# Linear attention emitted with neighbouring chunks turn by turn, constant rows filled by transfers, experts at an even rate

## The chip, the cores and the metric

The kernel runs on one core of one Trainium2 chip. The metric is the device time of one execution in microseconds (us). A core has a matmul engine (PE, its weight loads are shown as PEld), a vector engine (DVE), an activation engine (ACT), a general engine (POOL) and a queue from which this kernel starts all its transfers (SP). Each of them works through its own instructions in a fixed order and waits for the others by semaphores.

## The reference

x has the shape (4, 1024, 128): 4 sequences of T = 1024 tokens with 128 channels. Four layers follow one another; each reads a layer norm of x, and its output is added to x after a layer norm:

```python
x = x + _layernorm(_L0_attn_ref(_layernorm(x), ...))   # "A": time mixing by a scan, channel mixing
x = x + _layernorm(_L0_ffn_ref(_layernorm(x), ...))    # "B": 16 small experts, 4 per token, and a shared one
x = x + _layernorm(_L1_attn_ref(_layernorm(x), ...))   # "C": linear attention with decaying states
x = x + _layernorm(_L1_ffn_ref(_layernorm(x), ...))    # "D": softmax attention and 8 experts, 2 per token
```

Layer C is what the change is about. Per head (16 heads of 8 channels) and per time step it keeps two states M with decays b:

```python
M = M * b_t[:, :, None, None] + (k_t[:, :, None] * v_t[:, None, :])[:, None]
Z = Z * b_t[:, :, None] + k_t[:, None, :]
num = einsum('bd,bcde->be', q_t, M);  den = einsum('bd,bcd->b', q_t, Z) + EPS
y_t = num / den
```

## The kernel before

Channels lie on the 128 partitions, tokens along the free axis. The work of each layer is cut into chunks of 512 tokens, two per sequence, eight in all.

**Order of the work.** Stage A comes first, then stage B (the experts of the first feed-forward layer) beside stage C for sequences 0 and 1, then stage D, which is written out by hand and in which stage C of sequences 2 and 3 runs in between. The text is written as Python generators: each `yield` ends one step, and a driver takes steps from several generators in turn. Outside the hand-written last part the framework orders the instructions of each engine itself: the order of the text is a priority, and an instruction whose inputs and buffers are ready by the framework's own estimate may be put ahead of earlier text. Inside the last part the text order is the engine's order.

**Stage B.** `experts_b` gives 20 steps per sequence, ten per chunk; nine of the ten begin one expert: gate projection (`g_ps`, PE), clamp (L471, DVE), three activations (L473 to L475), two multiplications on POOL (L480 with the fetched routing weight, L481), the second projection (`u_ps`) with a product on DVE (L491), the third projection (`y_ps`, L464). Routing weights are fetched by one transfer per expert into three buffers (`gate`, L479). `STEPS_B = 10` of the 80 steps are written during stage A; the others are written by `with_experts` beside C and the heads of D: each "scans" step adds 0.28 to a count and each other step 0.1, and whenever the count passes 1 one expert step is written.

**Stage C**, `stage_c(b, pp, banks)`, per chunk:
- the front: the layer norm into `n2` (L573; one buffer), the projection v, written to memory as `v_rows` (L581), q and k with a rotation (`u` L588, `w` L591, sum on POOL L598, then `phi` L609) and the two decays `beta` (L596 to L610). The rotation table `turn` has a buffer of its own, fetched in one transfer of 512 KB (L569);
- the scans: for e in 8, 0, ..., 7 a product `kv` on POOL (L622, from a fetched row group `vrep`, three buffers, L618), two scans on DVE (L628), the sum of the two states on POOL (L638), a product with q on DVE (L642), and sums over partitions on PE (`den_ps` L668, `num_ps` L679);
- the tail: output projection (`o_ps` L690), `hh` (L693, in the buffer of `u`), two layer norms (L698, `ho` L704 in the buffer of `w`, L709), the sum into x (L712).

In this part of the kernel `beta` and `q` lie in three PSUM banks of their own; the other projections of C and of the heads share two PSUM banks (`room_c`).

**Ahead of D.** `keys_r` and `queries_r` (two tiles each) have constant rows 64 to 127, filled by POOL (L823, L824). `heads(b, h)` makes q, k and v of stage D, `spread(b, h)` moves them into place with 18 transfers.

The order written is: C of sequence 0 with experts (L795), the constants, heads and spread of sequence 0 for both chunks (L1237, L1238), C of sequence 1 with experts (L1239), what is left of the experts, stage D.

Of the kernel before, what the change touches and what calls it, by code (L numbers as in the profile page):

```python
# [11 lines left out]
FP = mybir.dt.float32  # L12
# [27 lines left out]
def sandwich(ctx: ExitStack, tc: tile.TileContext, x, vecs, cmats, rope, wa, wb, wc, wd, out):  # L40
# [509 lines left out]
    def stage_c(b, pp, banks=None):  # L550
# [4 lines left out]
        behind_c = pc.tile([P, 2, 9], FP, tag="behind_c", name="behind_c")  # L555
        for h in range(NH):
            c = chunk(h)
            n2 = pc.tile([P, CH], FP, tag="n2", name="n2", bufs=1)
            if banks is None:
                phi = [pc.tile([P, CH], FP, tag=f"phi{i}", name=f"phi{i}", bufs=1) for i in range(2)]  # L560
                beta = [pc.tile([P, CH], FP, tag=f"beta{i}", name=f"beta{i}", bufs=1) for i in range(2)]
            else:
                phi = [
                    banks.tile([P, CH], FP, tag="q", name="q_phi"),
                    pc.tile([P, CH], FP, tag="phi1", name="phi1", bufs=1),
                ]
                beta = [banks.tile([P, CH], FP, tag=f"beta{i}", name=f"beta{i}_ps") for i in range(2)]
            turn = pc.tile([P, 2, CH], FP, tag="turn", name="turn", bufs=1)
            nc.sync.dma_start(out=turn, in_=rope3[:, :, c])  # L569
            var = yield from mean_square_steps(pp, xT[b][:, c])  # L570
            rs = rstd(var, eps5)
            yield
            nc.vector.tensor_mul(n2, xT[b][:, c], rs)  # L573
            yield
            pv = project(pp, wv_c, n2, "v_ps")
            yield
            v = pc.tile([P, CH], FP, tag="o", name="v")
            nc.scalar.copy(v, pv)
            yield
            rows = dram.tile([P, CH], FP, tag="v", name="v_rows")  # L580
            nc.sync.dma_start(out=rows, in_=v)  # L581
            by_e = rows.rearrange("(h e) t -> e h t", e=8)
            for i in range(2):
                straight = project(pp, wqk[i], n2, "qk_ps")
                yield
                u = pc.tile([P, CH], FP, tag="u", name="u", bufs=1)
                w = pc.tile([P, CH], FP, tag="w", name="w", bufs=1)
                nc.vector.tensor_mul(u, straight, turn[:, 0, :])  # L588
                turned = project(pp, wrot[:, i, :], n2, "rot_ps")
                yield  # L590
                nc.vector.tensor_mul(w, turned, turn[:, 1, :])  # L591
                if banks is None:
                    pbt = project(pp, wbrep[:, i, :], n2, "beta_ps")
                else:
                    pbt = beta[i]
                    nc.tensor.matmul(pbt, lhsT=wbrep[:, i, :], rhs=n2, start=True, stop=True)  # L596
                yield
                nc.gpsimd.tensor_add(u, u, w)  # L598
                nc.vector.tensor_scalar(beta[i], pbt, vec(f"bbeta{i}"), -41.0, ALU.add, ALU.max)
                yield  # L600

                nc.vector.tensor_scalar_min(w, u, 0.0)
                nc.scalar.activation(beta[i], beta[i], AF.Exp, scale=-1.0)
                nc.scalar.activation(beta[i], beta[i], AF.Ln, bias=one)
                yield
                nc.scalar.activation(w, w, AF.Exp)
                nc.scalar.activation(beta[i], beta[i], AF.Exp, scale=-1.0)
                yield
                nc.vector.scalar_tensor_tensor(phi[i], u, 0.0, w, op0=ALU.max, op1=ALU.add)  # L609
                nc.vector.tensor_scalar(beta[i], beta[i], 0.001, 0.999, ALU.max, ALU.min)  # L610
                yield
            q, k = phi
            order = [8, 0, 1, 2, 3, 4, 5, 6, 7]
            values, kvs, sts, sums_e = {}, {8: k}, {}, {}

            def fetch(e):
                values[e] = pc.tile([P, CH], FP, tag="vrep", name="vrep", bufs=3)
                nc.sync.dma_start(out=values[e], in_=by_e[e].unsqueeze(1).to_broadcast([16, 8, CH]))  # L618

            def keyed(e):  # L620
                kvs[e] = pc.tile([P, CH], FP, tag="kv", name="kv")
                nc.gpsimd.tensor_mul(kvs[e], values.pop(e), k)  # L622

            def scan(e, i):
                if i == 0:
                    sts[e] = [state(m) for m in range(2)]
                before = behind_c[:, i, e : e + 1]
                nc.vector.tensor_tensor_scan(  # L628
                    sts[e][i], beta[i], kvs[e], before if h else 0.0, op0=ALU.mult, op1=ALU.add,
                )  # L630

            def add(e):
                s0, s1 = sts.pop(e)
                if h + 1 < NH:
                    for i, st in enumerate((s0, s1)):
                        nc.scalar.copy(behind_c[:, i, e : e + 1], st[:, CH - 1 : CH])
                sums_e[e] = [pc.tile([P, CH], FP, tag="qs", name="qs", bufs=5)]
                nc.gpsimd.tensor_add(sums_e[e][0], s0, s1)  # L638

            def times_q(e):  # L640
                for s_ in sums_e[e]:
                    nc.vector.tensor_mul(s_, s_, q)  # L642

            for e in range(3):
                fetch(e)
            os = []
            for n, e in enumerate(order + [None, None, None]):

                if n + 1 < len(order):
                    keyed(order[n + 1])  # L650
                if e is not None:
                    scan(e, 0)
                    yield "scans"
                    scan(e, 1)
                    if 0 <= e < 5:
                        fetch(e + 3)
                yield "scans"
                if 1 <= n <= len(order):
                    add(order[n - 1])
                yield "scans"  # L660
                if 2 <= n <= len(order) + 1:
                    times_q(order[n - 2])
                yield "scans"
                if n == 3:
                    den = pp([P, CH], "den_ps")
                    parts = sums_e.pop(8)
                    for m, s_ in enumerate(parts):
                        nc.tensor.matmul(den, lhsT=selden, rhs=s_, start=(m == 0), stop=(m == len(parts) - 1))  # L668
                    yield
                    qz = pc.tile([P, CH], FP, tag="qz", name="qz", bufs=1)  # L670
                    nc.scalar.activation(qz, den, AF.Ln, bias=eps6)
                    nc.scalar.activation(qz, qz, AF.Exp, scale=-1.0)
                if n in (7, 11):
                    part = n // 8
                    pn = pp([P, CH], "num_ps")
                    four = [sums_e.pop(4 * part + e4) for e4 in range(4)]
                    for m in range(len(four[0])):
                        for e4 in range(4):
                            nc.tensor.matmul(  # L679
                                pn[32 * e4 : 32 * e4 + 32, :], lhsT=into[:, part, :], rhs=four[e4][m],  # L680
                                start=(m == 0), stop=(m == len(four[0]) - 1),
                            )
                    yield
                    o = pc.tile([P, CH], FP, tag="o", name="o")
                    nc.vector.tensor_mul(o, pn, qz)
                    os.append(o)
            yield
            po = pp([P, CH], "o_ps")
            for i in range(2):
                nc.tensor.matmul(po, lhsT=wo_c, rhs=os[i], start=(i == 0), stop=(i == 1))  # L690
            yield
            hh = pc.tile([P, CH], FP, tag="u", name="hh", bufs=1)
            nc.vector.scalar_tensor_tensor(hh, po, bo_c, n2, op0=ALU.add, op1=ALU.add)  # L693
            yield
            var = yield from mean_square_steps(pp, hh)
            rs = rstd(var, eps5)
            yield
            nc.vector.tensor_mul(hh, hh, rs)  # L698
            yield
            yield  # L700
            pg = project(pp, gcenter, hh, "g_ps")
            yield
            ho = pc.tile([P, CH], FP, tag="w", name="ho", bufs=1)
            nc.scalar.activation(ho, pg, AF.Identity, bias=beta_c)  # L704
            yield
            var = yield from mean_square_steps(pp, ho)
            rs = rstd(var, eps5)
# [656 lines left out]
```

## Time and profile before

| what | value |
|---|---|
| time, median of 3 runs | 1582.55 us (1579.81 to 1585.23) |
| profiled execution, its time | 1582.11 us |
| its span | 1580.4 us |
| mean granted PE clock | 0.894 |
| busy: PE / DVE / ACT / POOL | 1222.9 / 1061.4 / 850.4 / 839.7 us |
| first C chunk begins (its squares, L543) | 310.3 us |
| first block of D (its row maxima, `sm`) begins | 689.4 us |

The page gives busy time per engine, the span in 40 slices, and the chain of work that ended last. "Busy" counts instructions as the profiler saw them; a share over the whole span mixes stages with different limits, so that each stage is read by itself. A row of windows gives for a stretch of time the busy time and the number of instructions of each engine, the granted PE clock (1 is full speed), the busy share of the transfer engines and the rate that they moved. A row of the timeline gives start, duration, engine, line, operation, output and inputs, and in brackets how long the engine had been idle and who released it.

### The profile page before, as it was taken

What the parts mean: (1) busy time and instruction counts of PE and PEld (TensorE: products, weight loads), DVE (VectorE), ACT (ScalarE), POOL (GpSimd) and SP (SyncE); (2) the same over time, 40 slices, a digit from 0 to 9 for tenths busy, and PEclk for the clock granted to TensorE, in tenths of its full rate; (3) what the DMA queues carried; (4) which work ended last, traced back from release to release, by engine and by line L of the source; (5) the groups of instructions that cost most, each with busy time, mean ns of one, the idle gap of its engine ahead of it and who ended that gap; (6) DMA issues with size and microseconds to landing.
All of it is one profiled execution on the core that took longest, in us unless ns stands there. A gap on an engine that the chain in (4) does not pass through costs nothing.

```text
span 1580.4 us, 15022 instructions
## 1 busy us (share of the span) xinstructions
PE 1222.9 (77%) x4524; PEld 443.9 (28%) x4532; DVE 1061.4 (67%) x1755; ACT 850.4 (54%) x1565; POOL 839.7 (53%) x901
## 2 busy tenths in 40 slices
PE   3457889948878678888779778867976889989864
PEld 1122333312323223233223223322322333333211
DVE  4556776557874686876996897698469766477501
ACT  3457777644537336446545456544663474756551
POOL 5555376596758556964453564462546454223312
PEclk8568999977879689999889899988998999999986
DMA  2000020231213413201203111312121113111102
GB/s 105 14 7 7 2 71 28 47 97 45 95 36 92 152 39 88 73 30 47 71 3 114 48 31 48 106 56 72 57 72 47 57 38 105 39 58 51 56 24 61
DMA packets 59329, 90.48 MB, mean 57 GB/s; under 512 B 9904, under 2 KB 26800, under 8 KB 58544
## 3 DMA queue, kind: packets, MB, share of 16 engines
q1 hardware_dynamic: 59248, 89.52, 19.1%
q8 instruction: 36, 0.59, 0.1%
q14 instruction: 45, 0.37, 0.1%
HBM read 76.38 MB, written 12.71 MB: 56 GB/s over the span
## 4 chain that ended last, share of the span: by engine, by line
PE 35%; DVE 23%; ACT 7%; POOL 4%; issue 4%; DMA 3%; SPq 2%; POOLq 0%; DVEq 0%; ACTq 0%
DVE st L628 7%; PE av L991 6%; PE sc L999 5%; DVE ms L935 4%; DVE ms L940 3%; PE y L1130 3%; PE ln_v L138 3%; ACT pr L1004 2%; PE sm L927 2%; PE sm L939 2%; PE g_ps L138 2%; PE u_ps L138 2%; DVE qs L642 2%; PE y_ps L464 2%; PE num_ps L679 1%
## 5 line engine op out<-in xcount | busy, mean ns | idle before, releaser
L1004 ACT ACTIVATE pr<-sc 128x512 f32<-128x512 f32 x576 | 328.0, 596 | 292.3 <-PE sc L999 285.1
L935 DVE TENSOR_REDUCE ms<-sm 128x1 f32<-128x512 f32 (+3 forms) x352 | 212.3, 633 | 108.5 <-PE sm L931 100.9
L999 PE MATMUL sc<-queries_r,keys_r 128*128 128x512 bf16 x576 | 223.4, 396 | 29.7 <-ACT pr L1004 27.9
L940 DVE TENSOR_REDUCE ms<-sm 128x1 f32<-128x512 f32 x256 | 166.3, 682 | 58.1 <-PE sm L939 57.9
L991 PE MATMUL av<-pr,va 128*32 128x512 f32 x1152 | 170.7, 648 | 3.6 <-POOL pr L1008 3.6
L927 PE MATMUL sm<-keys_r,queries_r 125*128 125x512 bf16 (+3 forms) x512 | 130.7, 312 | 43.1 <-DVE ms L935 35.4
L1008 POOL TENSOR_SCALAR_AFFINE_SELECT pr<-pr 128x512 f32<-128x512 f32 x128 | 95.2, 758 | 119.0 <-ACT pr L1004 118.5
L138 PE MATMUL ln_v<-rs,cm 128*128 128x512 f32 x176 | 106.8, 697 | 43.3 <-ACT rs L126 33.6
L1118 POOL TENSOR_TENSOR share<-n,every 128x512 f32<-128x512 f32 x64 | 80.5, 1273 | 99.2 <-DMA every<-row 79.6
L638 POOL TENSOR_TENSOR qs<-st,st 128x512 f32<-128x512 f32 x72 | 102.1, 1419 | 39.8 <-PE num_ps L679 14.9
L939 PE MATMUL sm<-keys_r,queries_r 125*128 125x512 bf16 x256 | 95.9, 398 | 22.9 <-DVE ms L940 19.7
L480 POOL TENSOR_TENSOR x<-x,gate 128x512 f32<-128x512 f32 x64 | 83.9, 1313 | 47.3 <-ACT g L473 43.5
L622 POOL TENSOR_TENSOR kv<-vrep,phi 128x512 f32<-128x512 f32 x64 | 87.2, 1365 | 40.9 <-issue 18.6
L481 POOL TENSOR_TENSOR g<-g,x 128x512 f32<-128x512 f32 x72 | 92.6, 1290 | 12.6 <-POOL x L480 6.5
L464 PE MATMUL y_ps<-g,wbt 128*128 128x512 f32 x144 | 78.9, 634 | 24.0 <-DVE g L491 23.7
L138 PE MATMUL g_ps<-n,wbt 128*128 128x512 f32 x144 | 83.2, 668 | 17.7 <-DVE x L471 8.1
L999 PEld LDWEIGHTS <-keys_r 128*128 128x128 bf16 x576 | 57.3, 101 | 129.8 <-issue 101.0
L491 DVE TENSOR_TENSOR g<-u_ps,g 128x512 f32<-128x512 f32 x72 | 49.5, 687 | 55.8 <-POOL g L481 34.6
L931 PE MATMUL sm<-later,identb 128*128 128x128 bf16 (+2 forms) x344 | 86.2, 251 | 0.0
L138 PE MATMUL u_ps<-n,wbt 128*128 128x512 f32 x144 | 77.5, 620 | 2.3 <-DVE x L471 1.3
L927 PEld LDWEIGHTS <-queries_r 125*128 125x128 bf16 x512 | 48.2, 101 | 108.2 <-issue 91.5
L473 ACT ACTIVATE g<-x 128x512 f32<-128x512 f32 x72 | 45.0, 626 | 56.1 <-DVE x L471 56.0
(302 smaller groups left out, 2357.5 us busy)
## 6 DMA issues: line engine op xcount, KB each, us to landing
gate<-rows SPq DMA_DIRECT2D x64, 256.0 KB
vrep<-v_rows SPq DMA_DIRECT2D x64, 256.0 KB
every<-row SPq DMA_DIRECT2D x64, 256.0 KB
queries_r<-dq SPq DMA_DIRECT2D x72, 128.0 KB
turn<-in_rope_dram SPq DMA_DIRECT2D x8, 512.0 KB
dq<-qp SPq DMA_DIRECT2D x8, 384.0 KB
keys_r<-dk SPq DMA_DIRECT2D x72, 32.0 KB
sums<-av_sb SPq DMA_DIRECT2D x128, 18.0 KB
```

Source lines behind the costliest of these rows:

```text
L138: nc.tensor.matmul(ps, lhsT=lhsT, rhs=rhs, start=True, stop=True)
L464: nc.tensor.matmul(py, lhsT=w, rhs=a, start=(w is w2s), stop=last)
L628: nc.vector.tensor_tensor_scan(sts[e][i], beta[i], kvs[e], before if h else 0.0, op0=ALU.mult, op1=ALU.add,)
L638: nc.gpsimd.tensor_add(sums_e[e][0], s0, s1)
L927: nc.tensor.matmul(view[:, k, :], lhsT=qr[0:MROWS, h, tb], rhs=kr[0:MROWS, half, h // 4, 0:n_s], start=(k == 0), stop=False, skip_group_ch ...
L935: nc.vector.tensor_reduce(ms[:, 0, h0 : h0 + in_bank], view, AX.X, ALU.max)
L939: nc.tensor.matmul(sc, lhsT=qr[0:MROWS, h, tb], rhs=kr[0:MROWS, 0, h // 4, :], start=True, stop=True)
L940: nc.vector.tensor_reduce(ms[:, 1, h : h + 1], sc, AX.X, ALU.max)
L991: nc.tensor.matmul(pavs[b, i][32 * g : 32 * g + 32, :], lhsT=va[:, j, g, :], rhs=pr, start=(j == 0), stop=(j == i),)
L999: nc.tensor.matmul(sc, lhsT=kr[0:ROWS, j // 4, g, j % 4 * P : (j % 4 + 1) * P], rhs=qr[0:ROWS, 4 * g : 4 * g + 4, tb], start=True, stop=True,)
L1004: nc.scalar.activation(pr, sc, AF.Exp)
L1008: nc.gpsimd.affine_select(out=every, in_=every, compare_op=ALU.is_ge, fill=0.0, base=0, pattern=[[0, 4], [1, P]], channel_multiplier=-1,)
```

## The change

1. `stage_c` is cut into `chunk_c(b, h, ...)`, which yields "front" after the front and "scanned" after the scans. The four chunks of sequences 0 and 1 are written thus: front and scans of chunk 0; then, for each next chunk, the tail of the chunk in front and the front of this one, one step of each in turn, and then the scans of this one. `stage_c` for sequences 2 and 3, inside stage D, calls `chunk_c` one after the other.
2. For that, `n2` has two buffers, `hh` and `ho` a buffer of their own, and `turn` is no longer a tile of its own: its two halves are two tiles of `vrep`'s three buffers, fetched by two transfers of 256 KB.
3. `heads(0, 0)` and `spread(0, 0)` are written in turn with the scans of chunk 1, `heads(0, 1)` and `spread(0, 1)` with those of chunk 2.
4. `STEPS_B` is 20, and the rates are 0.24 and 0.086 in place of 0.28 and 0.1.
5. Of the constant rows POOL fills one block of 512 elements per tile; a transfer from SP copies it to the other 15 (`queries_r`) or 7 (`keys_r`) blocks.

```diff
+    def chunk_c(b, h, pp, banks=None):
...
-            n2 = pc.tile([P, CH], FP, tag="n2", name="n2", bufs=1)
+        n2 = pc.tile([P, CH], FP, tag="n2", name="n2", bufs=2)
...
-            turn = pc.tile([P, 2, CH], FP, tag="turn", name="turn", bufs=1)
-            nc.sync.dma_start(out=turn, in_=rope3[:, :, c])
+        turn = []
+        for i in range(2):
+            turn.append(pc.tile([P, CH], FP, tag="vrep", name="turn", bufs=3))
+            nc.sync.dma_start(out=turn[i], in_=rope3[:, i, c])
...
+        yield "front"
...
+        yield "scanned"
         yield
...
-            hh = pc.tile([P, CH], FP, tag="u", name="hh", bufs=1)
+        hh = pc.tile([P, CH], FP, tag="hh", name="hh", bufs=1)
...
-            ho = pc.tile([P, CH], FP, tag="w", name="ho", bufs=1)
+        ho = pc.tile([P, CH], FP, tag="hh", name="ho", bufs=1)
...
-    GATES_B, STEPS_B = 8, 10
+    GATES_B, STEPS_B = 8, 20
...
-            beside[0] += 0.28 if step == "scans" else 0.1
+            beside[0] += 0.24 if step == "scans" else 0.086
...
-    with_experts(stage_c(0, room_c, pp_q))
+    def part(steps, last):
+        for step in steps:
+            yield step
+            if step == last:
+                return
+
+    def together(*several):
+        several = list(several)
+        while several:
+            for steps in list(several):
+                step = next(steps, "end")
+                if step == "end":
+                    several.remove(steps)
+                else:
+                    yield step
+
+    chunks_c = [chunk_c(b, h, room_c, pp_q) for b in range(2) for h in range(NH)]
+
+    def up_to_scanned(n, beside_scans=()):
+        if n == 0:
+            yield from part(chunks_c[0], "front")
+        else:
+            yield from together(chunks_c[n - 1], part(chunks_c[n], "front"))
+        yield from together(part(chunks_c[n], "scanned"), *beside_scans)
+
+    with_experts(up_to_scanned(0))
...
-        nc.gpsimd.memset(kr[64:128], -1.0)
-        nc.gpsimd.memset(qr[64:128], 0.0)
+        nc.gpsimd.memset(kr[64:128, 0, 0, :], -1.0)
+        nc.gpsimd.memset(qr[64:128, 0, :], 0.0)
+        first, others = qr[64:128, 0:1, :], qr[64:128, 1:16, :]
+        nc.sync.dma_start(out=others, in_=first.to_broadcast([64, 15, CH]))
+        kf = kr.rearrange("p a b t -> p (a b) t")
+        first, others = kf[64:128, 0:1, :], kf[64:128, 1 : NH * 4, :]
+        nc.sync.dma_start(out=others, in_=first.to_broadcast([64, NH * 4 - 1, CH]))
...
-    for h in range(NH):
-        with_experts(heads(0, h))
-        whole(spread(0, h))
-    with_experts(stage_c(1, room_c, pp_q))
+    def heads_and_rows(h):
+        yield from heads(0, h)
+        yield from spread(0, h)
+
+    with_experts(up_to_scanned(1, [heads_and_rows(0)]))
+    with_experts(up_to_scanned(2, [heads_and_rows(1)]))
+    with_experts(up_to_scanned(3))
+    with_experts(chunks_c[3])
     whole(all_experts)
```

## The prediction

> **What bounds the kernel now.** I read the page first, for the whole span:
>
> ```profile
> span 1580.4 us, 15022 instructions
> PE 1222.9 (77%) x4524; PEld 443.9 (28%) x4532; DVE 1061.4 (67%) x1755; ACT 850.4 (54%) x1565; POOL 839.7 (53%) x901
> PEclk8568999977879689999889899988998999999986
> ```
>
> No engine is full over the span; in the ninth and tenth slices PE has a low clock, so something else sets the pace there. I then cut the region of layers B and C into windows: at the first and last scans (L628) of each of the four C chunks, read from the timeline, and at the three places where a stage or a stall begins.
>
> ```profile
> core 0: us, PE busy (x) PEld busy (x) DVE busy (x) ACT busy (x) POOL busy (x), PEclk, DMA share, GB/s
> 327.00:345.00 18.00, 8.25 (x14) 2.94 (x14) 13.07 (x14) 9.21 (x16) 17.86 (x8) 0.78 0.10 31
> 345.00:377.00 32.00, 16.16 (x19) 2.34 (x19) 25.82 (x28) 6.95 (x25) 27.90 (x26) 0.50 0.21 65
> 377.00:409.00 32.00, 29.57 (x69) 11.93 (x66) 19.74 (x32) 20.40 (x34) 16.40 (x13) 0.98 0.29 90
> 409.00:455.00 46.00, 34.04 (x69) 10.71 (x67) 44.29 (x72) 16.27 (x27) 36.17 (x29) 0.76 0.18 58
> 455.00:512.00 57.00, 50.79 (x123) 19.73 (x122) 23.69 (x47) 38.66 (x69) 38.96 (x34) 0.96 0.28 71
> 512.00:527.00 15.00, 11.20 (x22) 4.56 (x22) 9.34 (x15) 7.67 (x13) 6.18 (x5) 0.89 0.46 144
> 527.00:538.00 11.00, 2.67 (x5) 0.62 (x3) 3.80 (x5) 1.70 (x4) 4.68 (x4) 0.55 0.63 180
> 538.00:580.00 42.00, 30.86 (x62) 9.81 (x62) 38.11 (x52) 17.62 (x41) 33.35 (x28) 0.75 0.25 82
> 580.00:630.00 50.00, 42.94 (x96) 16.19 (x97) 30.80 (x62) 30.08 (x51) 26.68 (x22) 0.97 0.27 68
> 630.00:672.00 42.00, 34.89 (x69) 10.94 (x68) 35.94 (x44) 19.57 (x31) 39.85 (x33) 0.95 0.24 76
> 302.00:691.00 389.00, 301.68 (x630) 104.53 (x629) 263.79 (x393) 194.51 (x352) 281.77 (x226) 0.86 0.27 78
> ```
>
> Two kinds of stretch alternate. In the scans (32, 46, 53 and 42 us, together 173) DVE and POOL are nearly full and PE is at half clock or idle. In the gaps between the scans of one chunk and the next (32, 72 and 50 us, together 154) PE is nearly full with experts and heads, and POOL is busy for half the time. Over 389 us the fullest engine by need is POOL, 281.8 us or 72%: no resource is full throughout, the two kinds of work merely take turns. In the third scans 11 us pass nearly empty (527 to 538): the 36 transfers of both spreads stand on SP ahead of `vrep`.
>
> The fill of the constants shows in the timeline of chunk 0's front:
>
> ```profile
> 319.20 6.92 POOL L824 MEMSET queries_r<- 64x8192 bf16 x1
> 326.20 1.26 POOL L598 TENSOR_TENSOR u<-u,w 128x512 f32<-128x512 f32 x1
> 327.52 3.51 POOL L823 MEMSET keys_r<- 64x4096 bf16 x1
> 330.97 7.20 POOL L824 MEMSET queries_r<- 64x8192 bf16 x1
> 338.25 1.27 POOL L598 TENSOR_TENSOR u<-u,w 128x512 f32<-128x512 f32 x1
> 327.50 3.81 DVE L602 TENSOR_SCALAR w<-u 128x512 f32<-128x512 f32 x1 [3.71 <-POOL u L598]
> ```
>
> L598 was ready when L591 ended, at 320.1 and 334.5: it stood 6.1 and 3.7 us behind fills; L602 took 3.81 us beside a fill against 0.43 elsewhere, 3.4 more. These rows show also that text order is not engine order: the fills are written after all of chunk 0 and 1, and ran before their scans.
>
> **The change part by part.** Sums are made on the profiled execution, 1582.1 us (span 1580.4); the median of three is 1582.55, so the two need no correction.
>
> *Ten more expert steps in stage A.* Of 72 experts the trace has 13 third projections (L464, two records each, 26 records) before 302 us; the 20 steps carry 18. So 5 experts move, each three projections of 0.86 us on PE (distance of back-to-back pairs at clock 1.00): 13 us. Between 190 and 302 us PE's row shows some 13 us of gaps. A's end thus moves by 0 (all in gaps) to 13 us (none); I take +6, the middle. DVE, ACT and POOL have 31, 36 and 26 of the last 52 us, so that PE alone decides.
>
> *Fills by transfer.* Removed: 21.2 us of POOL (2 x 3.5 + 2 x 7.06), of which 6.1 + 3.7 + 3.4 = 13.2 us lay in chunk 0's front. What replaces them on POOL is a sixteenth and an eighth, 1.8 us. Bounds 0 to -13; since POOL has expert products waiting that will take part of the room, I take -10. Added: transfers of 64 x 15 KB twice and 64 x 7 KB twice, 2.9 MB. They can be issued as early as the fills were, so ahead of `v_rows` (316 us) and three `vrep` and gate fetches on the same queue. At the rate of the window 500 to 540 (144 GB/s) they last 20 us, at the 260 GB/s that the view of transfers gives for 317 to 324 us, 11. The kv product needs `vrep` only two scans after phi, about 20 us after v; hence 0 to +20, taken +4.
>
> On that rate the Trainium skill ("SBUF — State Buffer", Door 1: The DMA port swizzle) speaks against the change: partitions 64 to 127 reach 8 of 16 ports, some 196 to 218 GB/s. By it the fills would last an estimated 13 to 15 us instead of 11, and the term would be +6. No transfer of this trace is confined to those partitions.
>
> *The gaps.* What must lie between the scans of two chunks is the longer of two chains, now side by side: the tail (chunk 0: 377 to the sum into x at 396, 19 us) and the front (chunk 1: squares at 390.5 to first scan at 409, 18.5 us). They were already overlapped by 6 us there, since only one n2 and the buffers of u and w bound them. Both share two PSUM banks, and with 11 projections held about 2.5 us each these two banks alone need 14 us. I take 20 per gap. Bounds: 11 (only the part of the front from the beta projection at 397.6 to the scan remains, the rest running inside the scans) and 32 (as the first gap now). The three gaps: 154 to 60, that is -94 (-121 to -58).
>
> *The scans take the experts that the gaps lose.* Counting yields, a chunk's scans write 11.1 expert steps and the heads 2.3 more in two of them: (4 x 11.1 + 4.6) x 0.9 / 4 = 11 experts per chunk. On POOL an expert costs 138 us / 57 = 2.42 us (rows L480 65.7 and L481 72.3), so 26.6; kv and the state sums, 17 x 1.27 = 21.6; a share of the heads (their products L828 to L830 and L864) 3.5, and the sums into x 1.6: 53.3 us. DVE needs less: 9 x 2.83 for two scans and a product, 11 x 1.2 for the experts, some 4 for routing, 43. The fourth scans reached 95% of POOL: 56 us. Bounds 53 (100%) to 67 (79%, as the second). Four scans: 173 to 224, +51 (+39 to +95). The empty 11 us go with them, as spread steps now alternate with scan steps, two transfers at a time.
>
> *The rest, at nothing.* `turn` loses its own buffer: its transfers wait until kv products of the chunk in front have freed `vrep`, two or three scans (5 us) before the gap, and are read by L588 about 9 us into the front; that cover is 14 us, and a rival below takes it away. `vrep` 1 and 2 of the next chunk wait for L591, some 5 us ahead of phi, and are needed two pairs of scans later. Two yields more per chunk in D's inserted chunks are 8 advances at 0.56 a tick, 14 of some 1200 ticks. It is charged with zero, -5 to +5. PE needs 0.86 us a projection at full clock and is not the bound in the scans.
>
> Sum: +6 - 10 + 4 - 94 + 51 = -43, so 1582.1 - 43 = **1539 us**. A second way: POOL's 281.8 us in the region, less 21 + 12 (five experts), plus 2, is 251; at 78%, the share of the second scans (36.17 of 46), the region lasts 322 us instead of 389, and with A's +6 it ends 61 earlier. The first sum is the more careful, and I keep it.
>
> **The rivals.**
> 1. *Work only changes place.* POOL holds 79% in all scans, as in the second: 67 us each, +95, and the gaps' -94 is gone: 1583. Between, at 86%, 62 us each: +75 - 94 = -19, 1563. For it: scan chains leave holes on POOL (the window of 538 to 580 has 79% as well). Against: the fourth scans at 95% with experts beside them. Range 1560 to 1583.
> 2. *The SP queue makes the front late.* SP works in order, and its waits show
>
> ```profile
> SPq L479 <- POOL x L480: 144.4, 37, 20.3
> ```
>
> that a gate fetch stood up to 20.3 us for a free gate buffer. `turn` had been fetched long ahead in a buffer of its own; now it must pass SP inside the scans, behind such waits, and so must the fills. The gain of 43 us is 14 us for each of three gaps: if `turn` lands over 14 us after it is wanted, the kernel is slower. At the 20.3 us it is 3 x 6 = 18 us slower, **1600**. Against: 37 waits sum to 144, so 4 us is usual.
> 3. *More gain*: fronts run inside the scans (gap 11 each, -27 more) and POOL is full in the scans (-12): 1500 to 1512.
> 4. *The change doesn't do what it says*: the framework reorders by readiness (the fills show it), and the turn-by-turn text makes the same engine order as before; then +6 - 10 + 4 = 0, 1582. Against: `n2`, `u` and `w` were held by the chunk in front, and that is lifted.
>
> **How the numbers follow.** Forecast 0.55 (1512 to 1560), rival 1 0.20, rival 2 0.14, rival 3 0.06, rival 4 0.05. A measurement of this kernel can tell 0.3%, 4.7 us, from no change. Faster: 0.55 + 0.06 + 0.17 of rival 1 = 0.78; within 0.3%: 0.02 of rival 1 and rival 4, 0.07; slower: 0.14 and 0.01 of rival 1, 0.15. The range leaves out rival 2, rival 4 and the end of rival 1: 1500 to 1580; the forecast's own is 1512 to 1560.
>
> **What would show it.** In the changed profile: the first block of D's maxima starts about 43 us earlier than 689.4; gaps between L628 groups near 20 us; scans near 56 us with POOL above 90% and PE's clock above 0.9 in them; no fill of over 0.5 us on POOL, L602 at 0.43 us; stage A's end (first C squares, 310.3) by 6 us later. The prediction is wrong if the gaps stay above 30 us, if scans last 67, if SP's waits stand ahead of `turn`, or if D from its first maxima to the end takes other than its 891 us by more than 5.

## The result and the profile after

The changed kernel took 1609.1 us in the median against 1583.9 us of the kernel before on the same chip: 1.0155 of its time, 95% interval 1.0135 to 1.0175, so 25 us slower where the forecast had 43 us less. The page of the profiled execution, span, busy time and PE's granted clock in 40 slices:

```profile
span 1606.3 us, 15026 instructions
PE 1231.9 (77%) x4524; PEld 449.3 (28%) x4532; DVE 1059.8 (66%) x1755; ACT 849.7 (53%) x1565; POOL 820.7 (51%) x901
PEclk8568899897888878999889999987998999999986
```

The work is the same (PE 1231.9 us against 1222.9, POOL 19 us less through the fills). PE's low slices in layer C have moved, not gone. The table by windows, cut at the scans (L634 now) and at the last product with q behind each group:

```profile
core 0: us, PE busy (x) PEld busy (x) DVE busy (x) ACT busy (x) POOL busy (x), PEclk, DMA share, GB/s
337.00:360.00 23.00, 17.50 (x38) 6.71 (x36) 11.40 (x20) 12.37 (x22) 16.80 (x26) 0.94 0.66 159
360.00:389.00 29.00, 19.00 (x24) 3.94 (x24) 27.53 (x31) 6.13 (x24) 22.31 (x18) 0.63 0.53 123
389.00:425.00 36.00, 28.67 (x72) 11.36 (x72) 27.91 (x64) 26.00 (x46) 19.16 (x16) 0.92 0.21 66
425.00:487.00 62.00, 42.51 (x97) 15.25 (x98) 41.06 (x55) 24.52 (x41) 42.27 (x36) 0.83 0.31 83
487.00:537.00 50.00, 36.44 (x68) 13.60 (x69) 21.78 (x33) 25.38 (x43) 24.49 (x21) 0.88 0.22 69
537.00:610.00 73.00, 52.76 (x118) 19.01 (x117) 55.47 (x91) 30.56 (x66) 47.91 (x40) 0.80 0.30 81
610.00:651.00 41.00, 33.47 (x64) 12.48 (x62) 19.66 (x31) 20.75 (x33) 22.98 (x20) 0.88 0.26 84
651.00:694.00 43.00, 33.92 (x71) 10.84 (x70) 38.34 (x46) 20.37 (x32) 41.47 (x34) 1.00 0.20 61
302.00:705.00 403.00, 305.17 (x635) 109.30 (x634) 259.44 (x390) 192.23 (x350) 259.20 (x224) 0.86 0.29 81
```

Gaps of 36, 50 and 41 us stand between groups of 29, 62, 73 and 43 us. POOL did lose its fills (259.2 us against 281.8) but holds 64% of the stretch, not 78%. Set side by side, with gaps counted from the end of a group's last product with q to the next group's first scan (the forecast's own cuts gave 173 us of scans and 154 us of gaps before), and D's first maxima taken as DVE's first reduction of `sm`, at 692.2 and 706.4 us (689.4, given for the kernel before, is the first weight load of that block):

| part | before, us | after, us | difference | forecast |
|---|---|---|---|---|
| end of stage A | 310.1 | 336.9 | +27 | +6 |
| A's end to the first scan | 34 | 23 | -11 | -6 |
| four groups of scans | 33 + 46 + 55 + 47 | 29 + 62 + 72 + 43 | +25 | +51 |
| three gaps | 32 + 72 + 45 | 36 + 50 + 41 | -22 | -94 |
| last product to D's first maxima | 18 | 12 | -5 | 0 |
| D's first maxima to the end | 888.2 | 899.9 | +12 | 0 |

The sum, +26, is the difference of the spans. Three places show what happened. In the second gap, the first projection on PE, and the timeline of DVE in chunk 2's front (n2, then the products with `turn`):

```profile
498.85 1.02 PE L138 MATMUL qk_ps<-n,wct 128*128 128x512 f32 x2
```

```profile
494.57 0.69 DVE L578 TENSOR_TENSOR n<-xT,ln_v 128x512 f32<-128x512 f32 x1 [2.26 <-ACT ln_v L121]
...
506.50 0.68 DVE L491 TENSOR_TENSOR g<-u_ps,g 128x512 f32<-128x512 f32 x1
507.09 0.68 DVE L471 TENSOR_SCALAR x<-g_ps 128x512 f32<-128x512 f32 x1
509.04 0.69 DVE L491 TENSOR_TENSOR g<-u_ps,g 128x512 f32<-128x512 f32 x1 [1.27 <-PE u_ps L138]
511.81 0.69 DVE L471 TENSOR_SCALAR x<-g_ps 128x512 f32<-128x512 f32 x1 [2.08 <-PE g_ps L138]
512.42 0.68 DVE L593 TENSOR_TENSOR u<-qk_ps,turn 128x512 f32<-128x512 f32 x1
...
526.97 0.69 DVE L593 TENSOR_TENSOR u<-qk_ps,turn 128x512 f32<-128x512 f32 x1 [0.17 <-PE qk_ps L138]
...
536.06 0.68 DVE L614 SCALAR_TENSOR_TENSOR phi<-u,w 128x512 f32<-128x512 f32 x1
```

PE had the first projection ready at 500; the product that reads it ran at 512, behind four instructions of experts on DVE's queue (L491 and L471, two of which themselves waited for PE), and the second projection's at 527. The front took 41 us from n2 to phi. In the third group, the timelines of SP and DVE:

```profile
578.11 0.65 SPq L949 DMA_DIRECT2D queries_r<-dq  x1
591.80 0.61 SPq L447 DMA_DIRECT2D rows<-comb  x1
...
593.14 1.78 SPq L945 DMA_DIRECT2D keys_r<-dk  x1
...
595.67 0.58 SPq L624 DMA_DIRECT2D vrep<-v_rows  x1
```

```profile
580.48 1.21 DVE L634 TENSOR_TENSOR_SCAN st<-beta_ps,kv 128x512 f32<-128x512 f32 x1
...
605.21 2.34 DVE L634 TENSOR_TENSOR_SCAN st<-beta_ps,kv 128x512 f32<-128x512 f32 x2
```

SP stood still from 578.8 to 591.8 at a write of routing rows, with transfers of the spread and the last `vrep` behind it; that `vrep` was issued at 595.7, its product ran at 603.9, and the last pair of scans began 23 us after the end of the one in front. SP's queue accounts for this hole up to 595.7. What held the product from there on is not shown: POOL stood until 600.8 at an instruction ahead of the product (L500, which waited for DVE).

The second group has a hole of much the same length (461.7 to 482.3), with another wait in it. From the timelines of SP, POOL and DVE:

```profile
460.76 0.58 SPq L624 DMA_DIRECT2D vrep<-v_rows  x1
477.00 1.28 POOL L628 TENSOR_TENSOR kv<-vrep,phi 128x512 f32<-128x512 f32 x1
482.31 2.45 DVE L634 TENSOR_TENSOR_SCAN st<-beta_ps,behind_c,kv 128x512 f32<-128x512 f32 x2
```

Here the last `vrep` was issued before the hole began, and its product came on POOL behind five products of experts (470.4 to 477.0). No row shows when the fetch landed. SP's waits from 302 to 705 us name the write of the third group (the second line shown), and the fetch of gates, 147 us in sum against 144 before:

```profile
SPq L479 <- POOL x L480: 147.2, 38, 14.2
...
SPq L447 <- ACT g L475: 13.5, 1, 13.5
```

### The profile page after: what moved, and what is told of

Its sections match the earlier page's. It is cut to its first block, busy times and chain, and to the rows that moved or that the text cites. A ratio compares the mean times of both kernels' runs of the same rounds, so it can differ in the third digit from the quotient of the medians.

```text
span 1606.3 us, 15026 instructions
## 1 busy us (share of the span) xinstructions
PE 1231.9 (77%) x4524; PEld 449.3 (28%) x4532; DVE 1059.8 (66%) x1755; ACT 849.7 (53%) x1565; POOL 820.7 (51%) x901
## 5 line engine op out<-in xcount | busy, mean ns | idle before, releaser
L1036 PE MATMUL av<-pr,va 128*32 128x512 f32 x1152 | 175.2, 660 | 3.6 <-POOL pr L1053 3.6
L138 PE MATMUL ln_v<-rs,cm 128*128 128x512 f32 x176 | 112.1, 728 | 40.1 <-ACT rs L126 29.8
L464 PE MATMUL y_ps<-g,wbt 128*128 128x512 f32 x144 | 82.0, 656 | 30.8 <-DVE g L491 30.8
L138 PE MATMUL g_ps<-n,wbt 128*128 128x512 f32 x144 | 79.5, 641 | 9.9 <-DVE x L471 6.5
L491 DVE TENSOR_TENSOR g<-u_ps,g 128x512 f32<-128x512 f32 x72 | 49.2, 684 | 41.5 <-POOL g L481 23.2
L471 DVE TENSOR_SCALAR x<-g_ps 128x512 f32<-128x512 f32 x72 | 49.2, 683 | 40.6 <-PE g_ps L138 40.3
```

Of the source, the lines that this page charges most:

```text
L138: nc.tensor.matmul(ps, lhsT=lhsT, rhs=rhs, start=True, stop=True)
L1036: nc.tensor.matmul(pavs[b, i][32 * g : 32 * g + 32, :], lhsT=va[:, j, g, :], rhs=pr, start=(j == 0), stop=(j == i),)
```

## The experiments

Each ratio is to the kernel before on the same chip; "us" behind it is the ratio's distance from 1 times 1582. The changed kernel stands at 1.0155, +25 us.

**The parts by themselves.** The pace undone in the changed kernel:

```
-    GATES_B, STEPS_B = 8, 20
+    GATES_B, STEPS_B = 8, 10
-            beside[0] += 0.24 if step == "scans" else 0.086
+            beside[0] += 0.28 if step == "scans" else 0.1
```

> The changed kernel with the old number of expert steps in stage A (10 in place of 20) and the old rates (0.28 and 0.1); turn-by-turn chunks, fills by transfer and the shared rotation buffer stay. Theory S (the experts written into stage A hold up its last chunks, and stage C cannot start before): stage A's last sum into x returns from 336.9 to about 310 us, and the kernel from 1609 to about 1582, or below it if the rest of the change is a gain. Theory T (the turn-by-turn text itself loses: spread transfers ahead of vrep, the rotation table late): A's end returns, but the C region grows by as much, and the time stays near 1605.

Measured 1601.4, ratio 1.0131 (1.0100 to 1.0162). A ends at 310.2 again, 27 us earlier, and the time follows by 4 us, which the two intervals do not tell from nothing. At this pace the gaps of the new order are 28, 70 and 63 us, 161 in sum, and the groups 35, 56, 53 and 48 us. The reverse edit in the kernel before:

> The kernel before with 20 expert steps in stage A and the rates 0.24 and 0.086, nothing else. Theory S: A's end moves from 310 to about 337 us; of this the 8 experts that are done earlier are given back in the C region only in part, so 1600 to 1611. Theory T: 20 us of A's delay come back in the C region, so 1584 to 1592.

1589.1, 1.0044 (1.0030 to 1.0058), +7 us. A's end comes at 337.3 there too. What is done earlier is given back afterwards but for 0 to 7 us. In layer C the new pace alone brings the gaps from 150 us to 140 and the groups of scans from 181 to 164.

The fills by transfer alone, in the kernel before (the diff's lines of that part):

> The kernel before with the constant rows filled by transfers, nothing else. From the changed profile, where front and fills took 11 us less from A's end to the first scan: 1570 to 1576 if the 11 us reach the end; 1584 if the scans of chunk 0 then wait for vrep behind the 2.9 MB, or if the experts only move.

1573.6, 0.9948 (0.9932 to 0.9963), -8 us. The first scan starts at 331 against 344. This part is a gain.

The chunks one after the other, all else as changed:

```
-    with_experts(up_to_scanned(0))
+    with_experts(chunks_c[0])
+    with_experts(chunks_c[1])
...
-    with_experts(up_to_scanned(1, [heads_and_rows(0)]))
-    with_experts(up_to_scanned(2, [heads_and_rows(1)]))
-    with_experts(up_to_scanned(3))
-    with_experts(chunks_c[3])
+    for h in range(NH):
+        with_experts(heads(0, h))
+        whole(spread(0, h))
+    with_experts(chunks_c[2])
+    with_experts(chunks_c[3])
```

> The changed kernel with the chunks of stage C written one after the other, and heads and spread of sequence 0 whole between them, as before; steps in A, rates, fills and buffers as changed. Theory T (turn by turn loses): 1585 to 1595, as only A's delay less the fills is left. Theory S (turn by turn is worth little or a few us): 1605 to 1620.

1584.2, 1.0022 (1.0001 to 1.0044), +4 us. The new order therefore costs 21 of the 25 us. In this kernel the gaps are 37, 64 and 39 us (140 in sum) and the groups sum to 162 us. At the same pace, then, the new order takes 13 us off the gaps and puts 44 us on the scans. What D pays for the two extra yields of a chunk, dropped where D goes through the second half of the batches:

```
-            yield from chunk_c(b, h, pp, banks)
+            for step in chunk_c(b, h, pp, banks):
+                if step not in ("front", "scanned"):
+                    yield step
```

> The changed kernel, but in stage D the two new yields of each inserted chunk (front, scanned) are taken without ending a step, so D's hand-written interleaving is that of before. Theory Y (the 8 extra steps push the inserted chunks and heads late in D): D from its first maxima to the end returns from 900 to 889 to 894 us, the kernel to 1595 to 1602. Theory B (D is longer because the rotation tables now share vrep's buffers there): D stays at 900 to 905, the kernel at 1609.

> Chunks of stage C one after the other, heads and spread whole between them, and D's steps as before; early experts, rates, fills and buffers as changed. Theory Y: 1570 to 1574, 11 us below the 1584 of the same kernel with the extra steps, faster than both kernels. Theory B: 1584.

In the changed kernel 1600.0, 1.0113 (1.0096 to 1.0131); with the chunks one after the other 1572.6, 0.9941 (0.9924 to 0.9958). The yields cost 7 and 13 us; D lasts 895.6 and 892.6 us where it lasted 899.9 and 905.1. The ratios carry this better than D's lengths, since D lasts 888.2 us in the kernel before and 893.1 and 893.8 with the pace or the fills alone, where its text is the same.

**The order, taken apart.** First, tail and front turn by turn, but heads and spread whole, behind the scans of chunks 1 and 2; second, the opposite, heads and spread among the scans, tail and front one after the other:

```
+    for h in range(NH):
+        with_experts(up_to_scanned(h + 1))
+        with_experts(heads(0, h))
+        whole(spread(0, h))
```

```
+    with_experts(chunks_c[0])
+    for h in range(NH):
+        with_experts(part(chunks_c[h + 1], "front"))
+        with_experts(together(part(chunks_c[h + 1], "scanned"), heads_and_rows(h)))
+        with_experts(chunks_c[h + 1])
```

> The changed kernel with tails and fronts turn by turn, but heads and spread of sequence 0 whole, behind the scans of chunk 1 and of chunk 2. If the loss of 25 us against chunks one after the other comes from heads and transfers among the scans: 1585 to 1592. If it comes from tails and fronts turn by turn: 1605 to 1612.

> The counterpart: chunks one after the other, heads and spread of sequence 0 turn by turn with the scans of chunks 1 and 2. If the loss comes from heads and transfers among the scans: 1605 to 1612. If it comes from tails and fronts turn by turn: 1583 to 1592.

The first took 1590.1, 1.0057 (1.0037 to 1.0076), +9 us; the second 1626.1, 1.0279 (1.0263 to 1.0295), +44. The second lies outside both ranges that were set for it. Turn by turn of tail and front is worth nothing without heads among the scans (+9 against +4) and 19 us with them (+25 against +44); heads with their spread among the scans cost 16 us in the new order (+25 against +9) and 40 in the old one (+44 against +4). The parts do not simply add up. Which of the two costs it, heads or spread? In the next kernel only heads stand among the scans, the spread's transfers behind them.

```
+    for h in range(NH):
+        with_experts(up_to_scanned(h + 1, [heads(0, h)]))
+        whole(spread(0, h))
```

> The changed kernel, but only the steps of heads go turn by turn with the scans of chunks 1 and 2; the 18 transfers of each spread are issued in one piece behind those scans. Theory (the transfers of the spread stand on SP's queue ahead of vrep, and the scans wait for vrep): the third group of scans goes from 73 us back to 50 to 58, and the time to 1588 to 1596, near the 1590 of the kernel that keeps heads and spread both behind the scans. Rival (it is the work of heads itself, on POOL, DVE and ACT among the scans, that costs): the third group stays at 65 us or more and the time at 1603 to 1612.

1588.1, 1.0053 (1.0028 to 1.0078), +8 us: all of the 16 come with the spread's transfers, and heads cost nothing there. The second and third groups last 53 and 47 us instead of 62 and 72. The gaps are 35, 66 and 39 us, 140 in sum, as with the chunks one after the other: beside the experts, tail and front turn by turn take nothing off them. Then the changed kernel with the spread issued from ACT's queue (`nc.scalar` in place of `nc.sync`):

> The changed kernel with the 36 spread transfers of the first batch issued from ACT's queue in place of SP's, in the same places of the order. Theory (it is their place ahead of vrep on SP's queue): the hole of 21 us in the third group of scans closes at least by half, and the time falls to 1588 to 1600. Rival (the transfers' own traffic, or the engines' work of heads, delays the scans whatever the queue): 1605 to 1615, since ACT now also stands still where a transfer waits for dk or dq.

1592.2, 1.0072 (1.0045 to 1.0099), +11 us. 13 of the 16 come back, but not where expected: the second group shrinks to 42 us and the third gap from 41 to 28, while the third group grows from 72 to 83 us. It has two holes now, with the last `vrep` long issued on SP: 23 us ahead of a pair of scans at 578.1, for which the trace names a copy on ACT (L642) as the last wait, and 15 us behind that pair, in which POOL waits 9.0 us for a product of layer B on DVE (L499). So the spread among the scans costs these us in the changed order, and its place on SP's queue is part of it. How large a part is not settled, since the framework orders POOL, DVE and ACT anew with each of these edits.

**Versions without the costly parts.** First the chunks one after the other at the old pace and without the yields in D. Then a new order, with the same two parts undone: tail, front, heads and spread all turn by turn in the gaps, nothing but experts among the scans:

```
+    with_experts(up_to_scanned(1))
+    for h in range(NH):
+        with_experts(together(chunks_c[h + 1], part(chunks_c[h + 2], "front"), heads_and_rows(h)))
+        with_experts(part(chunks_c[h + 2], "scanned"))
```

> Three of the four parts of the change undone: chunks one after the other with heads and spread between them, no extra yields where D goes through the second batch, experts at the old pace (10 steps, 0.28 and 0.1); the fills by transfers, the second buffer of n2 and the turn in vrep's buffers stay. If the costs found apart add up (1572.6 less the 7 to 8 of the earlier experts): 1562 to 1568, faster than the kernel before by 14 to 20. If the new pace has been hiding something in this order, or the two costs share a cause: 1570 to 1576, like the fills alone (1573.6).

> Tail and front turn by turn as in the change, but heads and spread of the chunk before go turn by turn with them, in the gaps between the groups of scans, none among the scans; old pace of the experts, no extra yields in D. If the turn-by-turn order of tail and front is worth something once the scans are left alone: gaps 2 and 3 at 40 to 55 us each against 72 and 50 of the kernel before, scans at 50 to 54 us, and 1548 to 1562. If the gaps are set by the engines' work and the waits in them, not by the chain of one chunk: gaps 60 to 75 us, and 1565 to 1580.

1573.0, 0.9938 (0.9919 to 0.9956), as with the fills alone: the old pace adds nothing in that order, and the second buffer of `n2` and the two tiles of `turn` among `vrep`'s, which this kernel keeps, cost nothing in it. The new order took 1568.0, 0.9915 (0.9888 to 0.9942), 13 us faster than the kernel before and 38 faster than the changed one by the ratios, the fastest of all that leave nothing out; its interval overlaps that of the one after the other, so its own share is not shown. Its windows, first three gaps, then the whole:

```profile
363.00:390.00 27.00, 27.00 (x62) 10.55 (x60) 18.62 (x30) 20.58 (x35) 15.36 (x13) 1.00 0.24 79
441.00:500.00 59.00, 52.46 (x120) 20.19 (x119) 30.77 (x52) 38.10 (x68) 35.78 (x31) 0.93 0.29 75
549.00:608.00 59.00, 49.95 (x115) 19.96 (x114) 34.15 (x71) 35.31 (x62) 35.21 (x31) 0.94 0.29 82
307.00:657.00 350.00, 274.86 (x579) 97.22 (x579) 254.01 (x381) 179.77 (x330) 252.38 (x219) 0.88 0.34 92
```

The gaps still sum to 145 us; PE is busy for 85 to 100% of each. The time is in the second of the ranges set for it, that of gaps set by the engines' work. The same with the spread on ACT's queue:

> The same kernel with the experts at their pace, and the 36 spread transfers issued from ACT's queue. If the order on SP still costs something where the spread stands in the gaps: 1556 to 1564. If it no longer does, or ACT's standing still costs as much: 1565 to 1575.

1587.7, 1.0039 (1.0026 to 1.0051), outside both ranges. 20 us are lost, where the same edit gained 13 in the changed kernel. ACT's waits say why:

```profile
ACT g L473 <- DMA keys_r<-dk: 36.7, 2, 22.4
```

ACT's arithmetic stood up to 22.4 us behind transfers in its own queue, from 627.6 to 650.0 us, during the fourth scans. These end at 652 us, but the experts that need ACT ran behind them: D's first maxima come 42 us later, where it is 13 us with the spread on SP's queue.

**Why the gaps stayed.** No step of the experts issued outside the scans (pace 0.4 or 0.34 beside them, 0 elsewhere), in the kernel before, in the changed one and in the order just shown:

> The kernel before with no step of the experts issued in the gaps between the groups of scans (pace 0.4 beside the scans, 0 elsewhere; in all as many). If the chain of tail and front alone fills the gaps, as the forecast had it: gaps stay at 33, 73 and 48 us within 5, and the scans get longer by what the experts add, 1590 to 1610. If the chain stands behind the experts on PE, DVE and ACT: gaps fall by some 10, 25 and 10 us (4, 11 and 4 experts of 2.6 us of PE each), the scans grow to 60 to 68 us each, and the time comes to 1575 to 1600.

> The changed kernel with no step of the experts issued in the gaps (pace 0.34 beside the scans, 0 elsewhere; in all as many). If the gaps of 36, 68 and 41 us are the two chains themselves: they stay within 5 us, and the time at 1605 to 1630. If they are the experts that stand on the queues between the steps of tail and front: gaps of 20 to 35 us, scans of 60 to 80 us since POOL was busy there at 0.75 to 0.95 already, and 1590 to 1612.

> The kernel with tail, front, heads and spread turn by turn in the gaps, with no step of the experts there (pace 0.4 beside the scans, 0 elsewhere). Chains alone: gaps stay at 28, 55 and 52 us, and 1575 to 1595. Experts in the way: gaps at 20, 35 and 35 us, scans at 60 to 68 us, and 1555 to 1575.

1593.2 (1.0078, 1.0050 to 1.0106), 1627.8 (1.0283, 1.0265 to 1.0301) and 1573.6 (0.9941, 0.9922 to 0.9959). The gaps are 40, 75 and 44 us, 31, 54 and 52, and 29, 54 and 61: in sum the same or 10 us longer. But the experts were not kept out of them. PE's third projections (L464) in the three gaps, of the quiet kernel and then of the kernel before:

```profile
378.00:418.00 40.00, 6.99 (x14) 2.66 (x14) 0.98 0.26 86
462.00:536.00 74.00, 15.39 (x28) 5.28 (x28) 0.94 0.31 86
595.00:639.00 44.00, 10.47 (x20) 3.47 (x20) 0.99 0.23 78
```

```profile
377.00:409.00 32.00, 7.78 (x15) 2.96 (x16) 0.98 0.29 90
455.00:527.00 72.00, 13.20 (x26) 4.61 (x26) 0.94 0.32 86
583.00:628.00 45.00, 8.36 (x16) 2.88 (x16) 0.99 0.30 76
```

As many ran there (62 records against 57; in the other two 35 against 36 and 56 against 52), issued during the scans and late from them. So these three said nothing on the cause, and two more left the 70 steps out altogether in stage C (63 of 72 experts by the records of L464), once in the old order and once in the changed one at the old pace:

```
-            beside[0] += 0.28 if step == "scans" else 0.1
+            beside[0] += 0.0
...
-    whole(all_experts)
```

> The kernel before without the 70 steps of the experts that it issues beside the linear attention of the first two batches (they are left out altogether; the 10 in stage A stay). If the gaps hold the experts' work that the scans leave over: PE's work between A's end and the first maxima falls from 295 us to about 110, the gaps from 32, 72 and 45 us to 20 to 27, 45 to 60 and 25 to 35, the scans from 46 to 55 us to 36 to 46, and D begins 60 to 110 us earlier. If the gaps are the chain of tail and front with its own waits: they fall by less than 5 us each.

> The changed kernel at the old pace, without the same 70 steps of the experts. If the experts' work is what kept the gaps from closing: gaps of 15 to 25 us, as the forecast had them, and D begins 30 to 60 us earlier than in the kernel before without those steps. If the order itself gains nothing (the chains wait for each other, or SP's queue for heads): gaps above 30 us, a third group of scans still longer than the others by 15 us, and D begins within 15 us of the other.

1473.7 us, 0.9321 (0.9289 to 0.9353), and 1433.5 us, 0.9064 (0.9040 to 0.9088). Windows of the gaps, old order and then new:

```profile
360.00:390.00 30.00, 15.92 (x26) 5.25 (x24) 10.95 (x17) 11.58 (x19) 3.79 (x3) 0.76 0.15 52
418.00:471.00 53.00, 30.98 (x54) 10.98 (x52) 13.48 (x27) 21.61 (x37) 17.93 (x17) 0.65 0.21 68
508.00:540.00 32.00, 17.89 (x30) 5.72 (x26) 11.27 (x18) 11.58 (x19) 3.79 (x3) 0.71 0.10 33
```

```profile
352.00:376.00 24.00, 17.34 (x31) 5.17 (x28) 11.47 (x19) 13.06 (x23) 4.18 (x4) 0.78 0.12 44
407.00:434.00 27.00, 18.38 (x57) 7.24 (x54) 15.28 (x25) 14.21 (x24) 5.40 (x8) 0.92 0.21 72
465.00:491.00 26.00, 14.61 (x30) 4.37 (x26) 11.55 (x19) 10.79 (x18) 3.88 (x4) 0.83 0.23 75
```

Without the experts the order does nearly what the forecast had: gaps of 24, 27 and 26 us against 30, 53 and 32, groups of scans of 27 to 32 us though heads and spread run among two of them, and no hole. The last product with q ends at 518 us against 568. Of these 49 us, 11 are the fills, ahead of the first scan (322 against 333); some 9 are lost again behind the last product, and the time is 40 us less. (In both kernels D's first maxima already run among the chunks, at 478.5 and 425.9 us, so some of the room that the experts leave is taken by D.)

The experts turn that round: they add 108 us in the old order (1581.5 less 1473.7), and in the new one at the same pace 168 (1601.4 less 1433.5). PE's busy time over the whole span, old order and then new, shows what they need:

```profile
PE 1059.8 (72%) x4050; PEld 373.7 (25%) x4058; DVE 936.7 (64%) x1503; ACT 714.1 (49%) x1331; POOL 682.6 (46%) x775
```

```profile
PE 1048.2 (73%) x4050; PEld 371.7 (26%) x4058; DVE 932.8 (65%) x1503; ACT 712.3 (50%) x1331; POOL 666.3 (47%) x775
```

That is 163 us in the old order (1222.9 less 1059.8) and 180 in the new one at the same pace (1227.9 less 1048.2). So in the old order some 55 us of the experts' PE work cost no time, and in the new one next to none. The plain reading is that this work ran in time that the chunks left idle, and that the new order closes just that time. With the experts the gaps of the new order at that pace go from 77 us in sum to 161, those of the old one from 115 to 150.

## Why the prediction was wrong, step by step

- **The gaps, -94: the step that failed.** "What must lie between the scans of two chunks is the longer of two chains", taken at 20 us. This is nearly right for the chains (24 to 27 us without experts) and wrong for the kernel: with the experts the gaps were 36, 50 and 41 us, only 22 us less than before, and 10 of these come with the new pace alone. Where only the spread is taken out of the scans, they are as long as with the chunks one after the other, 140 us in both. The sum asked for some 289 us of PE work (302 less the 13 moved into stage A) in a stretch of 389 - 43 = 346 us, 84%, and "PE needs 0.86 us a projection at full clock and is not the bound in the scans" passed that over. The measured shares are 78% before, 76% after, and 79% in the best version.
- **The scans, +51: right in sign, wrong in cause.** "The scans take the experts that the gaps lose" had 11 experts in each of four groups, 44 in all. By the records of L464 (two for each expert) some 27 ran in them, against 21 before, and 18 stayed in the gaps. The groups grew by 25 us (by 44 against the old order at the same pace), and by no greater load on POOL, which held 42.27 of 62 and 47.91 of 73 us in the long groups where the forecast had 95%: the growth lies in the second and third, which have the holes shown above. "Two transfers at a time" was thought to remove the 11 empty us of the old third group; it spread the 36 transfers among the fetches of `vrep`. Taking them out of the scans gave 16 us back.
- **Rival 2** had the right queue for one of the two holes and nearly the right time (1600), but that was luck: it priced `turn` at gate waits, where in the third group `vrep` stood behind the spread and the write of routing rows, and in the second gap both halves of `turn` were issued by 494 us, well ahead of the product at 512. **Rival 1** ("work only changes place") describes the gaps and stopped at 1583, since it had no new wait in it.
- **Stage A, +6: mis-sized.** It ends 27 us later: 7 experts more ran before chunk 0's n2, not 5 (46 records of L464 against 32), 7 x 2.58 = 18 us of PE, so none of it was hidden in PE's gaps; the other 9 us are not explained. The forecast set the 18 experts written with the new steps against the 13 that had run by 302 us, though only 9 were written there before (18 records in the kernels without the later 70 steps): the framework had taken the others ahead of their text, and did so again. In the time it is worth 0 to 7 us.
- **Fills, -10 + 4: right.** -8 us alone, POOL's fills down to pieces of 0.52 us, L607 back at 0.43 us. The rule of the Trainium skill quoted there ("SBUF — State Buffer", Door 1: The DMA port swizzle) is not decided (the 196 GB/s is measured there on partitions 0 to 63, as many ports): the fills travelled among other transfers, at 159 and 123 GB/s in the windows 337 to 360 and 360 to 389, and no run has them alone.
- **D, charged at zero: a missed cost.** 7 to 13 us. The estimate was at hand: 14 ticks of some 1200 in 890 us are 10 us, and nothing in the profile spoke for D having that room. Two of the signs that the prediction set for its own failure thus came true, gaps above 30 us and a D longer by more than 5.

In sum, from the ratios and for the changed order: fills -8, yields in D +7 to +13, pace 0 to +7, spread among the scans +16, and tail and front turn by turn +5, where the two intervals still touch. In another order the same parts cost otherwise, as the +44 shows. What the experts wait for, engine by engine, when the order closes their room is not settled.

## What to carry to other kernels

Before two stretches are folded into each other, add up each engine's work over both and divide by the time that the forecast leaves; and ask what runs for nothing in the idle time to be closed, since leaving that filler out is the test that tells whether it is the chain or the filler. A transfer that is moved among urgent ones is priced by what stands ahead of it in its queue, the waits of unrelated work too. A yield added to a generator that something else steps through is a tick of that schedule: price it at the schedule's time per tick.

## What was not expected of the hardware

The queue that issues a transfer mattered with both signs. The Trainium skill ("DMA: Bandwidth & Descriptors", Rules for kernel authors) holds that spreading transfers over several issuing engines brings no bandwidth and saves issue time only. No run here measures that bandwidth. What the runs show is that the waits in a queue count for more than its issue time: the same 36 transfers on ACT's queue gained 13 us in the order where SP had stood 13.5 us at one write, and lost 20 us in the order where ACT then stood 22.4 us at a transfer.
